# Graph network kernel: zeros of two one-hot tiles by VectorE at the program's start, one input load moved into the preparation, the last count stores on two queues

## The chip, the cores and the metric

The kernel runs on one core of a Trainium2 chip. The metric is the device time of one execution in microseconds, lower being better. Before the change it is 4598.26 us, the median of three runs (4597.88 to 4599.86). A shorter wall time on this one core is all that counts.

The core has five engines that run side by side and wait for each other by semaphores: TensorE (PE, matrix multiplication), VectorE (DVE), ScalarE (ACT), GpSimd (POOL) and SyncE (SP). SP, ACT and POOL also issue DMAs. An engine works through its own instructions in order, so an instruction that waits holds up everything behind it on that engine.

## The reference, cut to what matters

There are 6250 nodes with 128 features (x) and 206250 directed edges (src, dst), sorted by dst. Two layers follow each other, each with a residual and a layer norm:

```
deg  = segment_sum(1, col);  dinv = rsqrt(deg);  w = dinv[row] * dinv[col]
x_out = 0.1 * x;  h = x
for 5 times:  h = segment_sum(h[col] * w, row);  x_out += 0.18 * h
x = layernorm(x + x_out @ weight.T + bias)          # layer 0: propagation
x = layernorm(x + edge_attention(x, edge attributes))  # layer 1: 8 heads, softmax per dst node
```

The change touches only what comes before and at the start of layer 0's five rounds.

## The kernel before, in words

Nodes are held in 49 tiles of 128. Edges are padded to 206336 and laid out so that 1612 of them lie on each of the 128 partitions. The work has four stages, in this order.

**Preparation** (in `gnn_kernel`, lines 1168 to 1243). x goes to the tile `hs` (line 1170), the edges' ends and attributes to SBUF and to DRAM scratch (`srct`, `dstt`, `eat`). DVE makes bf16 one-hot tiles of the destinations (`one_hot`, line 153) and PE multiplies them into the number of edges of each node (line 1206). From this come `cnt`, `first` (the first edge of a node) and `dinv`. Here the framework's scheduler sets the order on each engine.

**Counting** (`count_rows`, lines 158 to 269). It makes a dense matrix of uint8 counts, destination by source, in DRAM (`counts`). POOL gathers the sources of every node's edges by 49 indirect DMAs (line 178), one a node tile. Then POOL writes zeros over the off-diagonal halves of two one-hot tiles `oh_los` (lines 185 and 186), two memsets a tile. These stay zero: for each tile t, DVE writes only the two diagonal blocks of `oh_los[t % 2]` and the whole of `oh_hi`. The loop over t runs in an order written out by hand for PE, DVE and ACT, in a software pipeline: `split` (seven tiles at a time, DVE), `turn` (PE transposes, ACT copies them out), `hot` (DVE one-hots), `count` (64 matmuls into PSUM, line 228, that ACT casts into `cT`, line 230), `put` (DVE transposes `cT` into `c_row`, line 236, adds the self loop, line 243, and SP stores it in 16 DMAs, line 249). `cT` and `c_row` have two buffers each. POOL is not in that hand-written order: after the gathers and the memsets it scales `hs` by `dinv` (line 1253, seven instructions, one of which runs ahead of the gathers).

**The sums** (`propagate`, lines 272 to 465). Five rounds; in each, four quarters of the destination nodes; in each, all 49 source tiles. SP loads two tiles' counts at a time into `c8` (line 419, five buffers). DVE (line 427) and ACT (lines 432 to 440) cast them to fp32r, and PE multiplies them by `parts`, the split `hs` (line 444). `parts` is made by ACT (line 415) and DVE (line 416) during the first quarter of each round. Ahead of all this, ACT issues three loads: `xo` (x again, 3.2 MB, line 287), the weight `wT` (line 288) and the bias (line 289), and scales `wT` (line 290). `xo` is first used when a quarter's sums are finished (line 329). A side job, one step per source tile, orders the nodes and lays out the edges for the next stage.

**Attention** (`attend`), which neither the diff nor the prediction's steps touch.

Each DMA issued by SP or ACT signals one of eight completion counters, which the scheduler hands out in turn over both queues; a DMA waits until the last one on its counter has landed.

Of the kernel before, what the change touches and what calls it, by code (L numbers as in the profile page):

```python
# [7 lines left out]
F32 = mybir.dt.float32  # L8
BF = mybir.dt.bfloat16
FR = mybir.dt.float32r  # L10
U8 = mybir.dt.uint8
# [7 lines left out]
P = 128  # L19
N = 6250  # L20
NT = 49
# [12 lines left out]
D = 128  # L34
# [11 lines left out]
Q = 4  # L46
# [3 lines left out]
H4 = 25  # L50
# [104 lines left out]
        table[:, None, :n, :].to_broadcast([p, b, n, Q]), OP.is_equal)  # L155


def count_rows(tc, first, cnt, srct, tab_lo, tab_hi, iota, ident_b, counts):

    nc = tc.nc
    with tc.tile_pool(name="cr1", bufs=1) as one, tc.tile_pool(name="cr2", bufs=2) as two, \
            tc.tile_pool(name="cr_t", bufs=1, space=PSUM) as pt, \
            tc.tile_pool(name="cr_c", bufs=6, space=PSUM) as pc:
        src = one.tile([P, NT, SLOTS], I32, name="src_e")
        low = one.tile([P, 7, SLOTS], I32, name="low_e")  # L170
        high = one.tile([P, 7, SLOTS], I32, name="high_e")
        ok = one.tile([P, 7, SLOTS], F32, name="ok_e")

        lh = one.tile([P, NT, 4, SLOTS], BF, name="lh")
        at = one.tile([P, NT], I32, name="at_e")
        nc.vector.tensor_copy(at, first)
        for t in range(NT):
            nc.gpsimd.indirect_dma_start(
                out=src[:, t, :], out_offset=None, in_=srct[:, :],
                in_offset=bass.IndirectOffsetOnAxis(ap=at[:, t:t + 1], axis=0))  # L180
        oh_los = [one.tile([P, 64 // Q, P, Q], BF, name=f"oh_l{i}") for i in range(2)]
        cTs = [one.tile([P, H4, 64, 4], U8, name=f"cT{i}") for i in range(2)]
        for i in range(2):

            nc.gpsimd.memset(oh_los[i][:64, :, 64:, :], 0.0)
            nc.gpsimd.memset(oh_los[i][64:, :, :64, :], 0.0)
        turned = {}

        def split(c):

            x = slice(c, c + 7)
            nc.vector.tensor_tensor(ok, iota[:, None, :SLOTS].to_broadcast([P, 7, SLOTS]),
                                    cnt[:, x, None].to_broadcast([P, 7, SLOTS]), OP.is_lt)
            nc.vector.tensor_single_scalar(low, src[:, x], 63, OP.bitwise_and)
            nc.vector.tensor_single_scalar(high, src[:, x], 6, OP.logical_shift_right)
            nc.vector.tensor_copy(lh[:, x, 0:2], low[:, :, None, :].to_broadcast([P, 7, 2, SLOTS]))

            for i in (2, 3):
                nc.vector.scalar_tensor_tensor(lh[:, x, i], ok, -float(P), high, op0=OP.mult, op1=OP.add)

        def turn(t):

            p_t = pt.tile([P, 2, P], BF, name="p_lh")
            for i in range(2):
                nc.tensor.transpose(p_t[:, i, :], lh[:, t, 2 * i:2 * i + 2].rearrange("p a j -> p (a j)"),
                                    ident_b)
            turned[t] = two.tile([P, 2, 64], BF, name="lhT")
            for a in range(2):
                y = slice(64 * a, 64 * a + 64)
                nc.scalar.copy(turned[t][y], p_t[y, :, y])  # L210

        def hot(t):

            v = turned.pop(t)
            for a in range(2):
                y = slice(64 * a, 64 * a + 64)
                one_hot(nc, oh_los[t % 2][y, :, y, :], v[y, 0, :], tab_lo[y], 64)
            oh_hi = two.tile([P, 64 // Q, 4 * H4, Q], BF, name="oh_h")
            one_hot(nc, oh_hi, v[:, 1, :], tab_hi, 4 * H4)
            return oh_hi  # L220

        def count(t, oh_hi):
            cT = cTs[t % 2]
            for q0 in range(0, 64, 5):
                n = min(5, 64 - q0)
                p_c = pc.tile([P, 5, 4 * H4], F32, name="p_c")
                for q in range(q0, q0 + n):
                    nc.tensor.matmul(p_c[:, q - q0], oh_los[t % 2][:, q // Q, :, q % Q],  # L228
                                     oh_hi[:, q // Q, :, q % Q], start=True, stop=True)
                nc.scalar.copy(cT[:, :, q0:q0 + n, :].rearrange("p h q m -> p q h m"),  # L230
                               p_c[:, :n].rearrange("p q (h m) -> p q h m", m=4))

        def put(t):

            c = two.tile([P, 2, H4, 32, 4], U8, name="c_row")
            nc.vector.transpose(  # L236
                c.rearrange("p n h l m -> p (n h l m)").bitcast(F32).rearrange(
                    "p (n h l) -> p n h l", n=2, h=H4),
                cTs[t % 2].rearrange("p h q m -> p (h q m)").bitcast(F32).rearrange(
                    "p (h n i) -> p n h i", n=2, h=H4))  # L240
            m = 2 * ((t + 1) % 2)
            own = c[:, :, (t + 1) // 2, :, m:m + 2]
            nc.vector.tensor_tensor(own, own, ident_b.rearrange("p (m n l) -> p n l m", m=2, n=2), OP.add)
            for a in range(2):
                for b in range(2):
                    y = slice(64 * a + 32 * b, 64 * a + 32 * b + 32)
                    for q, (h0, h1) in enumerate(H4S):
                        w = (h1 - h0) * P
                        nc.sync.dma_start(
                            bass.AP(tensor=counts.tensor,  # L250
                                    offset=counts.offset + (t * P + 64 * a) * HR + 2 * h0 * P + b * w,
                                    ap=[[HR, 32], [32 * HR, 2], [1, w]]),
                            c[y, :, h0:h1].rearrange("p n h l m -> p n (h l m)"))

        with tc.manual_schedule(engines=MANUAL):
            hots = {}
            for t in range(-2, NT + 1):
                if 0 <= t + 2 < NT:
                    if t == -2:
                        split(0)  # L260
                    if (t + 2) % 7 == 3 and t + 6 < NT:
                        split(t + 6)
                    turn(t + 2)
                if 0 <= t + 1 < NT:
                    hots[t + 1] = hot(t + 1)
                if 0 <= t < NT:
                    count(t, hots.pop(t))
                if 0 <= t - 1 < NT:
                    put(t - 1)


def propagate(tc, x, hs, wT0, b0, counts, ident, dinv, x1_d, x1_r, rank_i, side):

    nc = tc.nc
    tiled = "(t p) d -> p t d"
    with tc.tile_pool(name="pr1", bufs=1) as one, tc.tile_pool(name="pr2", bufs=2) as two, \
            tc.tile_pool(name="pr3", bufs=3) as three, tc.tile_pool(name="pr4", bufs=4) as four, \
            tc.tile_pool(name="pr_t", bufs=1, space=PSUM) as pt, \  # L280
            tc.tile_pool(name="pr_a", bufs=7, space=PSUM) as pa:
        xo = one.tile([P, NT, D], F32, name="xo")
        parts = one.tile([P, NT, 2, D], FR, name="parts")
        wT = one.tile([P, D], F32, name="wT")
        bias = one.tile([P, D], F32, name="bias")

        nc.scalar.dma_start(xo, x.rearrange(tiled, p=P))
        nc.scalar.dma_start(wT, wT0)
        nc.scalar.dma_start(bias, rows_of(b0, 0, D))
        nc.scalar.mul(wT, wT, ALPHA)  # L290
# [5 lines left out]
        side = side(spare)  # L296
# [106 lines left out]
        with tc.manual_schedule(engines=MANUAL):  # L403
            for k in range(K):
                for q, (t0, t1) in enumerate(QUARTERS):
# [6 lines left out]
                    for j0 in range(0, NT, 2):  # L412
# [9 lines left out]
                        for j in range(j0, j0 + m):  # L422
                            c = four.tile([P, WQ], FR, name="c")
# [703 lines left out]
def gnn_kernel(ctx, tc, x, srcf, dstx, srcp, dstp, easT, eas, wT0, b0, wq, wdot, w1, b1,  # L1127
               wang, w2, wlin, wout, c_ident, c_iota, c_count, c_dump, c_upto, c_before,
               c_heads, c_sum, out):
    nc = tc.nc  # L1130
# [4 lines left out]
    counts = dram.tile([NT, P, HR], U8, name="counts")  # L1135

    srct = dram.tile([EP, 1], I32, name="srct")
# [5 lines left out]
    x1_d = dram.tile([NP, D], F32, name="x1_d")  # L1143
    x1_r = dram.tile([NP, D], F32, name="x1_r")
# [4 lines left out]
    ident = glob.tile([P, P], F32, name="ident")  # L1149
    nc.sync.dma_start(ident, c_ident)  # L1150
    dinv = glob.tile([P, NT], F32, name="dinv")
    has = glob.tile([P, NT], F32, name="has")
    last = glob.tile([P, NT], I32, name="last")
    cnt = glob.tile([P, NT], F32, name="cnt")
# [12 lines left out]
    with ExitStack() as s:  # L1167

        hs = s.enter_context(tc.tile_pool(name="hs1", bufs=1)).tile([P, NT, D], F32, name="hs")
        nc.scalar.dma_start(hs, x.rearrange("(t p) d -> p t d", p=P))  # L1170
        prep_s = s.enter_context(ExitStack())
        prep = prep_s.enter_context(tc.tile_pool(name="prep", bufs=1))
        work_s = prep_s.enter_context(ExitStack())
        work = work_s.enter_context(tc.tile_pool(name="prep_w", bufs=1))

        dst_i = prep.tile([P, NC], I32, name="dst_i")
        nc.sync.dma_start(dst_i, dstp)
# [4 lines left out]
        nc.sync.dma_start(srct, srcf)  # L1182
        nc.sync.dma_start(dstt, dstx)
        nc.scalar.dma_start(eat, eas)


        tab_lo = prep.tile([P, P, Q], BF, name="tab_lo")
# [60 lines left out]
                                  skip_runtime_bounds_check_because="a count of partitions")  # L1248
        with tc.If(unsorted > 0):
            sort_edges(tc, dram, srcf, dstx, eas, dst_i, first, iota, ident, c_before, srct, dstt, eat)  # L1250
        count_rows(tc, first, cnt, srct, tab_lo, tab_hi, iota, ident_b, counts)
        for c in range(0, NT, 7):
            nc.gpsimd.tensor_tensor(hs[:, c:c + 7], hs[:, c:c + 7],
                                    dinv[:, c:c + 7, None].to_broadcast([P, 7, D]), OP.mult)
# [8 lines left out]
                                   rank_i, flag2)  # L1263
            yield from lay_edges(tc, one, two, rows, srct, eat, src_all, eas_o)

        propagate(tc, x, hs, wT0, b0, counts, ident, dinv, x1_d, x1_r, rank_i, side)
    attend(tc, w1, b1, wang, w2, wlin, wqd, wout, ident, rows, c_iota, src_all, eas_o, x1_d, x1_r, out)
    more = nc.values_load(flag2[0:1, 0:1], min_val=0, max_val=P,
                          skip_runtime_bounds_check_because="a count of partitions")
# [79 lines left out]
```

## Time and profile before

| what | value |
|---|---|
| median of three runs | 4598.26 us |
| the profiled execution, its own time | 4606.73 us |
| its span, first to last instruction | 4604.9 us |
| PE busy | 3785.5 us, 82% of the span |
| DVE busy | 3751.0 us, 81% |
| ACT busy | 2051.8 us, 45% |
| POOL busy | 2353.1 us, 51% |
| granted TensorE clock, mean | 0.931 |

The table of windows has one row for a stretch of the span: busy microseconds of PE, of the weight loads (PEld), of DVE, ACT and POOL, each with its number of instructions, then the granted clock, the DMA engines' busy share and GB/s. By stage it reads, in busy time of the three engines named:

| stretch, us | stage | PE | DVE | POOL | granted clock |
|---|---|---|---|---|---|
| 0 to 206 | preparation, first one-hots | 87.21 | 175.26 | 19.85 | 1.00 |
| 206 to 263 | counting, its start | 0.18 | 11.29 | 46.22 | 1.00 |
| 365 to 465 | counting, in its steady course | 59.67 | 99.10 | 0.00 | 0.66 |
| 785 to 850 | from counting to the sums | 40.91 | 38.58 | 1.58 | 0.79 |
| 850 to 930 | the sums | 80.00 | 73.11 | 0.00 | 1.00 |

A line of the timeline gives the start, the duration, the engine (a "q" behind it is the engine's queue, issuing a DMA or waiting), the line of the kernel, the operation, output<-input with shapes, and how many such instructions were merged; in brackets stands the idle time before it and what ended that.

### The profile page before, as it was taken

To read this page: it belongs to the slowest core of one execution; us is meant where nothing else is said; L and a number is where in the kernel's file an instruction comes from. 1 tells how busy PE (TensorE), PEld (TensorE's weight loads), DVE (VectorE), ACT (ScalarE), POOL (GpSimd) and SP (SyncE) were. 2 spreads that over 40 slices of the span, in tenths; PEclk is the share of its full clock that TensorE was granted. 3 is DMA by queue.
4 is the path that set the end of the run, shared out by engine and by line. 5 is a ranking of instruction groups with operands and counts; after the bars stand their busy time and mean duration, and the time that the engine had idled before them with its cause. 6 is when DMAs were issued, how large, how long until landed. Compare 5 with 4: busy or idle time off the path is not lost.

```text
span 4604.9 us, 73118 instructions
## 1 busy us (share of the span) xinstructions
PE 3785.5 (82%) x24823; PEld 3371.9 (73%) x24823; DVE 3751.0 (81%) x5996; ACT 2051.8 (45%) x4137; POOL 2353.1 (51%) x2343
## 2 busy tenths in 40 slices
PE   4345554997999999999868898987888878888886
PEld 4345554886888888787667788887888868787785
DVE  8769996865787787766649898987988988899887
ACT  0046664644656566464334343443443433444333
POOL 0340000056333344303277777777777777777774
PEclk9986766998999999999989999999999999999898
DMA  8023334555877788765365455554555555555442
GB/s 296 9 50 78 80 78 115 150 155 164 238 229 229 222 233 247 230 174 155 111 125 101 98 102 101 103 99 97 102 100 100 106 97 105 102 103 102 90 100 48
DMA packets 389736, 601.64 MB, mean 131 GB/s; under 512 B 120093, under 2 KB 325205, under 8 KB 378554
## 3 DMA queue, kind: packets, MB, share of 16 engines
q1 hardware_dynamic: 256570, 356.98, 32.0%
q0 software_dynamic: 127056, 204.67, 19.4%
q10 hardware_dynamic: 5728, 35.22, 2.3%
q8 instruction: 201, 3.29, 0.3%
q14 instruction: 181, 1.48, 0.1%
HBM read 491.89 MB, written 132.25 MB: 136 GB/s over the span
## 4 chain that ended last, share of the span: by engine, by line
PE 23%; DVE 11%; DMA 8%; POOL 7%; issue 5%; ACT 1%; SPq 0%; DVEq 0%; POOLq 0%; ACTq 0%
DMA xs<-x_d,src_all 7%; PE p_r L850 6%; POOL xs L788 6%; PE p_k L866 5%; PE p_k L864 3%; DVE mkv L839 3%; DVE kv L871 3%; PE acc L444 3%; PE p_g L831 2%; PE p_x L817 1%; DVE kv L902 1%; DVE kv L909 1%; DVE kv L873 1%; PE p_h L831 1%; POOL x_r L368 1%
## 5 line engine op out<-in xcount | busy, mean ns | idle before, releaser
L788 POOL DMA_INDIRECT xs<-x_d,src_all x1658 | 1676.7, 1011 | 505.5 <-issue 423.1
L444 PE MATMUL acc<-c,parts 128*128 128x512 f32 (+1 forms) x6370 | 1411.1, 382 | 78.9 <-DVE c L427 42.8
L444 PEld LDWEIGHTS acc<-c,parts 128*128 128x128 f32 x6370 | 1154.3, 189 | 305.8 <-DVE c L427 48.9
L427 DVE CAST c<-c 128x1024 fp32r<-128x1024 uint8 x980 | 683.8, 716 | 240.1 <-PE acc L444 196.2
L866 PE MATMUL p_k<-wlin_s,mkv 128*128 128x128 f32 x3316 | 755.4, 310 | 0.0
L440 ACT CAST c<-c 128x512 fp32r<-128x512 uint8 x735 | 456.2, 623 | 561.5 <-PE acc L444 441.9
L864 PE MATMUL p_k<-wlin_s,mkv 128*128 128x64 f32 x3316 | 581.1, 258 | 65.7 <-DVE kv L871 64.8
L850 PE MATMUL p_r<-w_s,r 128*128 128x192 f32 x3316 | 619.9, 330 | 0.0
L850 PEld LDWEIGHTS p_r<-w_s,r 128*128 128x128 f32 x3316 | 571.2, 194 | 34.4 <-issue 0.2
L864 PEld LDWEIGHTS p_k<-wlin_s,mkv 128*128 128x128 f32 x3316 | 523.1, 199 | 95.0 <-DVE kv L871 94.1
L871 DVE TENSOR_TENSOR kv<-rr,p_k 128x768 f32<-128x768 f32 (+2 forms) x443 | 397.1, 898 | 205.6 <-PE p_k L866 189.0
L854 ACT COPY rr<-p_r 128x768 f32<-128x768 f32 (+2 forms) x443 | 335.3, 759 | 476.8 <-PE p_r L850 462.2
L839 DVE TENSOR_TENSOR mkv<-p_g,xT 128x512 f32<-128x512 f32 (+3 forms) x866 | 534.2, 659 | 7.0 <-PE p_g L831 6.9
L866 PEld LDWEIGHTS p_k<-wlin_s,mkv 128*128 128x128 f32 x3316 | 523.5, 199 | 0.0
L228 PE MATMUL p_c<-oh_h,oh_l 128*128 128x100 bf16 x3136 | 301.1, 273 | 263.3 <-DVE oh_h L153 199.5
L833 ACT ACTIVATE r<-p_h,b_s 128x512 f32<-128x512 f32 (+3 forms) x433 | 290.6, 671 | 464.1 <-PE p_h L831 456.4
L228 PEld LDWEIGHTS <-oh_l 128*128 128x128 bf16 x3136 | 289.3, 124 | 272.2 <-DVE oh_h L153 208.0
L668 POOL DMA_DIRECT2D eas_o<-eT_l x252 | 204.9, 816 | 505.2 <-DVE eT_l L662 490.7
L817 PE MATMUL p_x<-ident,xs 128*128 128x128 f32 x1658 | 276.9, 279 | 131.7 <-DMA xs<-x_d,src_all 123.2
L230 ACT CAST cT<-p_c 128x500 uint8<-128x500 f32 (+1 forms) x637 | 306.8, 644 | 118.1 <-DVE c_row L236 61.1
L817 PEld LDWEIGHTS p_x<-ident,xs 128*128 128x128 f32 x1658 | 212.2, 142 | 164.4 <-DMA xs<-x_d,src_all 122.6
L820 ACT COPY xT<-p_x 128x512 f32<-128x512 f32 (+3 forms) x433 | 248.6, 574 | 135.9 <-PE p_x L817 131.9
(195 smaller groups left out, 4524.8 us busy)
## 6 DMA issues: line engine op xcount, KB each, us to landing
c<-counts SPq DMA_DIRECT2D x360, 384.0 KB
ea<-eas_o SPq DMA_DIRECT2D x648, 128.0 KB
c<-counts SPq DMA_DIRECT2D x120, 448.0 KB
eas_o<-eT_l POOLq DMA_DIRECT2D x162, 256.0 KB
counts<-c_row SPq DMA_DIRECT2D x588, 48.0 KB
xs<-x_d,src_all POOLq DMA_INDIRECT x1658
eat<-in_eas ACTq DMA_DIRECT2D x1, 25792.0 KB
counts<-c_row SPq DMA_DIRECT2D x196, 56.0 KB
```

The costliest lines, as they stand in the source:

```text
L228: nc.tensor.matmul(p_c[:, q - q0], oh_los[t % 2][:, q // Q, :, q % Q], oh_hi[:, q // Q, :, q % Q], start=True, stop=True)
L427: nc.vector.tensor_copy(c[:, u:u + 1024].rearrange("p (n b x) -> p n b x", n=2, b=2), r[:, :, v:v + 512].rearrange("p b (n x) -> p n b x", ...
L440: nc.scalar.copy(c[:, 1024:w].rearrange("p (b x) -> p b x", b=2), r[:, :, 512:])
L444: nc.tensor.matmul(a[:, :v - u], parts[:, j, i, :], c[:, u:v], start=(j == 0 and i == 0), stop=(j == NT - 1 and i == 1))
L788: nc.gpsimd.indirect_dma_start(out=xs[g][:, i, :], out_offset=None, in_=x1_d[:, :], in_offset=bass.IndirectOffsetOnAxis(ap=src_all[:, c:c ...
L817: nc.tensor.transpose(p_x[:, i * P:(i + 1) * P], xs[g][:, i, :], ident)
L839: nc.vector.tensor_tensor(mkv[g][:, i, :n].rearrange("p j (b e) -> p b j e", b=4), p_g[:, i, :n * P].rearrange("p (b j e) -> p b j e", b=4 ...
L850: nc.tensor.matmul(p_r[:, i // 2, u:u + DK + D], r[:, i, :], w2_s, start=True, stop=True)
L854: nc.scalar.copy(r2[:, b, :f], p_r[:, b, :f])
L864: nc.tensor.matmul(p_k[:, i // 2, u:u + DK], m[:, 0, i, :], wlin_s[:, :DK], start=True, stop=True)
L866: nc.tensor.matmul(p_k[:, i // 2, u + DK:u + DK + D], m[:, 1, i, :], wlin_s[:, DK:], start=True, stop=True)
L871: nc.vector.tensor_mul(k.rearrange("p (b i) f -> p b (i f)", b=b.stop - b.start), r2[:, b, :f], p_k[:, b, :f])
```

## The change

Three edits are made.

1. The two `oh_los` tiles move out of `count_rows` into the preparation's pool, and their four zero memsets are issued by DVE instead of POOL, in the program's text ahead of all loads of the edges. `count_rows` gets the tiles as an argument.
2. `xo` moves out of `propagate` into a pool of its own beside `hs`. Its load stands in the preparation, on ACT's queue behind the load of `eat`.
3. `c_row` gets three buffers instead of two. Of the last tile's 16 stores (t = 48), the eight of the second half of the partitions (a = 1) are issued by ACT, the others by SP as before.

```
-def count_rows(tc, first, cnt, srct, tab_lo, tab_hi, iota, ident_b, counts):
+def count_rows(tc, first, cnt, srct, oh_los, tab_lo, tab_hi, iota, ident_b, counts):
...
-        oh_los = [one.tile([P, 64 // Q, P, Q], BF, name=f"oh_l{i}") for i in range(2)]
         cTs = [one.tile([P, H4, 64, 4], U8, name=f"cT{i}") for i in range(2)]
-        for i in range(2):
-
-            nc.gpsimd.memset(oh_los[i][:64, :, 64:, :], 0.0)
-            nc.gpsimd.memset(oh_los[i][64:, :, :64, :], 0.0)
...
-            c = two.tile([P, 2, H4, 32, 4], U8, name="c_row")
+            c = two.tile([P, 2, H4, 32, 4], U8, name="c_row", bufs=3)
...
-                        nc.sync.dma_start(
+                        (nc.scalar if a and t == NT - 1 else nc.sync).dma_start(
...
-        xo = one.tile([P, NT, D], F32, name="xo")
-        nc.scalar.dma_start(xo, x.rearrange(tiled, p=P))
...
         nc.scalar.dma_start(hs, x.rearrange("(t p) d -> p t d", p=P))
+        xo = s.enter_context(tc.tile_pool(name="xo1", bufs=1)).tile([P, NT, D], F32, name="xo")
...
+        oh_los = [prep.tile([P, 64 // Q, P, Q], BF, name=f"oh_l{i}") for i in range(2)]
+        for o in oh_los:
+            nc.vector.memset(o[:64, :, 64:, :], 0.0)
+            nc.vector.memset(o[64:, :, :64, :], 0.0)
...
         nc.scalar.dma_start(eat, eas)
+        nc.scalar.dma_start(xo, x.rearrange("(t p) d -> p t d", p=P))
```

In the order of instructions that the scheduler gives the changed kernel, the following differs on the engines. On DVE the four memsets are the first, third, fourth and fifth instruction, and a memset of `ones` and one table operation come a little later. On ACT the load of `xo` stands between those of `eat` and `upto` (a constant that PE needs at the end of the preparation). At the end of counting, ACT's queue has the loads `wq_s`, `wd_s` and `wT`, then the eight stores, then a few small copies, the bias and the scaling of `wT`, and only then the first copy into `parts`. On POOL the memsets are gone, and two loads of x blocks for the last round come ahead of four small set-up operations instead of behind them. Everything else has the same order on all engines.

More of the change, by code (lines that the diff above doesn't have):

```diff
@@ L269, in count_rows, with propagate @@
                     put(t - 1)
-def propagate(tc, x, hs, wT0, b0, counts, ident, dinv, x1_d, x1_r, rank_i, side):
+def propagate(tc, x, hs, xo, wT0, b0, counts, ident, dinv, x1_d, x1_r, rank_i, side):
     nc = tc.nc
@@ L1250, in gnn_kernel @@
             sort_edges(tc, dram, srcf, dstx, eas, dst_i, first, iota, ident, c_before, srct, dstt, eat)
-        count_rows(tc, first, cnt, srct, tab_lo, tab_hi, iota, ident_b, counts)
+        count_rows(tc, first, cnt, srct, oh_los, tab_lo, tab_hi, iota, ident_b, counts)
         for c in range(0, NT, 7):
@@ L1264, in side @@
             yield from lay_edges(tc, one, two, rows, srct, eat, src_all, eas_o)
-        propagate(tc, x, hs, wT0, b0, counts, ident, dinv, x1_d, x1_r, rank_i, side)
+        propagate(tc, x, hs, xo, wT0, b0, counts, ident, dinv, x1_d, x1_r, rank_i, side)
     attend(tc, w1, b1, wang, w2, wlin, wqd, wout, ident, rows, c_iota, src_all, eas_o, x1_d, x1_r, out)
```

## Prediction

> **What bounds the kernel now.** I read the page first (82% PE, 81% DVE: no engine is full, so stages differ), then the table of windows by stage, then the list of waits, longest first in total, then the timeline at the seams between stages. Two seams stand out. The list of waits (engine and line, who ended it, total us, times, longest) has the first:
>
> ```profile
> PE p_c L228 <- POOL oh_l L186: 63.8, 2, 62.9
> DVE oh_l L153 <- PE p_c L228: 51.7, 1, 51.7
> ```
>
> PE once waits 62.9 us for a POOL memset, and DVE once 51.7 us for the matmuls behind it. The timeline shows where:
>
> ```profile
> 198.19 4.61 DVE L153 TENSOR_TENSOR oh_l<-lhT,tab_lo 64x4096 bf16<-64x4096 bf16 x2 [0.68 <-ACT lhT L210]
> 203.92 3.22 POOL L178 DMA_INDIRECT src_e<-srct,at_e  x1 [0.30 <-issue]
> 206.24 4.60 DVE L153 TENSOR_TENSOR oh_l<-lhT,tab_lo 64x4096 bf16<-64x4096 bf16 x2
> 214.27 0.62 DVE L192 TENSOR_TENSOR ok_e<-iota,cnt 128x448 f32<-128x448 f32 x1
> 216.21 1.14 DVE L199 SCALAR_TENSOR_TENSOR lh<-ok_e,high_e 128x448 bf16<-128x448 f32 x2
> ...
> 254.73 0.95 POOL L178 DMA_INDIRECT src_e<-srct,at_e  x1 [0.30 <-issue]
> ...
> 262.82 6.17 PE L228 MATMUL p_c<-oh_h,oh_l 128*128 128x100 bf16 x64 [62.94 <-POOL oh_l L186]
> 269.09 5.99 DVE L153 TENSOR_TENSOR oh_l<-lhT,tab_lo 64x4096 bf16<-64x4096 bf16 x2 [51.74 <-PE p_c L228]
> 269.95 18.60 POOL L1253 TENSOR_TENSOR hs<-hs,dinv 128x896 f32<-128x896 f32 x6
> ...
> 306.34 4.59 DVE L153 TENSOR_TENSOR oh_l<-lhT,tab_lo 64x4096 bf16<-64x4096 bf16 x2
> ```
>
> DVE has the one-hots of tiles 0 and 1 ready at 214.35 and the next split done at 217.35. Then it is idle until 269.09, because PE may not start tile 0's matmuls before POOL's memsets, and POOL reaches those only after 49 gathers. From 304 on DVE is 99% busy at 10.12 us a tile (306.34 to 316.46: 4.6 for oh_l, 3.5 for oh_h, 1.84 transpose, 0.3 add), while PE is busy 60%: counting is bound by DVE, so an earlier start of DVE is an earlier end, one for one. The second seam:
>
> ```profile
> 769.78 18.74 SPq L249 DMA_DIRECT2D counts<-c_row  x40
> ...
> 775.10 1.84 DVE L236 STREAM_TRANSPOSE c_row<-cT 128x1600 f32<-128x1600 f32 x1 [6.74 <-DMA counts<-c_row]
> ...
> 790.08 2.64 SPq L419 DMA_DIRECT2D c<-counts  x5
> ...
> 791.05 16.55 ACTq L288 DMA_DIRECT2D wT<-in_wT  x1
> ...
> 808.13 0.41 ACT L415 CAST parts<-hs 128x256 fp32r<-128x256 f32 x1 [17.96 <-issue]
> ...
> 809.09 3.22 PE L444 MATMUL acc<-c,parts 128*128 128x384 f32 x7 [35.97 <-DVE parts L416]
> ...
> 811.63 0.31 ACT L290 ACTIVATE wT<-wT 128x128 f32<-128x128 f32 x1 [2.08 <-DMA wT<-in_wT]
> ```
>
> SP issues the count stores at 18.74/40 = 0.47 us each; the last starts at 788.1, and the sums' first load goes out at 790.08. ACT issues the load of xo, then needs 16.55 us to issue the small wT behind it, and only then makes the first parts, without which PE cannot start (809.09). It stalls once more at 811.63 for wT itself. After that PE is busy 100% (850 to 930) and nothing in the chain to the end depends on a time before this seam.
>
> **The change part by part.**
>
> *Zeros off POOL.* PE can start tile 0 when oh_h of tile 0 is there (its second DVE operation ends near 206.2), and finishes by 213 (its 64 matmuls take 6.17). DVE's next one-hot then starts at 217.35 instead of 269.09: **51.7 us gained**. The cover that is lost: what POOL did while DVE stood idle now runs beside a full DVE. 32 gathers are left at 215.5. Beside one-hots they took 1.9 to 3.2 us instead of 0.95, seven of them 16.8 us (198.64 to 215.48), 2.4 each with the gaps. So they end near 215.5 + 32 x 2.4 = 292 and not 255. The split that needs gather 20 comes at t = 8, near 217 + 7 x 10.1 = 288; gather 20 is out by 225. Nobody waits. The one-hots were not slowed by the gathers (4.61 and 4.60 at 198 and 206, 4.59 alone at 306). They are slowed by POOL's scaling of hs (5.99 and 7.46 instead of 4.6): from 269.09 the two tiles beside it took 14.15 and 12.98, that is 6.9 us over 2 x 10.12. The same six instructions will meet a full DVE again, later, so the 6.9 us stay in both. Here the Trainium skill speaks against the change: "SBUF — State Buffer", section "The single rule", says VectorE and GpSimd share a port pair by an exclusive lock, a VectorE operation with two SBUF inputs blocking a GpSimd one that reads SBUF for its whole length. By the rule a gather could wait out a whole one-hot (3.5 + 1.25 = 4.7 us), 32 of them until 366; gather 20 would still be out by 235, so the answer is the same. For the six scalings the rule allows 6 x 1.72 = 10.3 us of blocked DVE, against 6.9 in the row. I take the row; bounds: 3.4 lost, 6.9 gained.
>
> *Zeros on DVE.* They cost DVE time at the start of the program, where the timeline has this:
>
> ```profile
> 30.75 1.84 DVE L1238 TENSOR_TENSOR viol<-dflat,dprev 128x1612 f32<-128x1612 int32 x1 [10.61 <-DMA dprev<-in_dstx]
> ```
>
> DVE's chain has 10.6 us to spare there. The built memsets write 2048 four-byte elements each. Nearest row: DVE's memset of 128 in 0.165 us, so at most 4 x 2048 x 1.29 ns = 10.6 us; "VectorE: DVE Perf Modes", section "Zero memsets can be issued as uint32", has one cycle an element, 4 x 2.13 = 8.5 us as an estimate. They start at 0.84; ident_b (0.23) comes among them, tab_lo (0.43) after them, and the first operation on dst_i (6.30 now) starts near 10.2, with tab_hi and ones (0.44) behind it: some 4.4 us late, inside the 10.6. **Nothing** on the path. A gain is excluded, as nothing else starts earlier; were the memsets twice as long (4096 elements), 17 to 21 us would push the chain 2 to 6 us past that wait. Taken 0, bounds 0 and 6 lost.
>
> *xo's load moved.* In the preparation its row-wise descriptors (6272 of 512 B) queue behind eat, whose last packets end at 109.9. At the 325 GB/s of that stretch, 3.2 MB need 10 us more. ACT stands in its issue meanwhile, as it did for 16.47 us behind hs, and upto waits behind it. upto is wanted at 178.7 and ACT's next work at 179.2, so all lands with 50 us to spare; without that cover it would be the 16.5 us. DVE's wait for dprev is not touched: dprev is ahead of eat.
>
> At the seam ACT's path loses 790.15 to 807.6. What is late next is the counts load: the DMA completions in the trace have the first c8 load land at 793.96, 3.88 us after its issue, and xo's packets started only at 794.0, so this is its own time. From ACT's first cast of c8 to PE's first matmul it is 809.09 - 808.44 = 0.65 us. PE starts 4.5 us after that load's issue: 794.6 if stores end as before, **14.5 us gained**. wT, now issued before the last stores, will have landed; the stall at 811.63 delayed the second source tile (PE's first seven matmuls take 3.22 instead of 1.52 for a source tile), so **1.6 us** more. Bounds 12 and 19. POOL's two x loads move ahead of rec_o's set-up; in the built program they wait for no store, so DVE's first use of rec_o is not held up.
>
> *The last stores.* Tile 48's DVE transpose waits 6.74 us for a c_row buffer now; with three it starts at 771.8, when ACT's last cast is done, and ends at 773.9. SP's chain of 0.47 us stores is not shortened by that: it ran without a gap. What shortens it is eight stores less, 8 x 0.47 = 3.8 us. But in the built program SP's seventh store of tile 47 waits on the completion counter of ACT's sixth store. ACT issues wq_s, wd_s, wT from 771.9 and its stores from 774.0; fifth and later wait for the first to land (last store at 788.1, landing seen at 789.8: 1.7 us each), so the sixth lands near 778.1, and SP, due at 776.4, loses 1.7. **2.1 us gained.** The skill's "DMA: Bandwidth & Descriptors", section "Issuing engines are not separate DMA queues", says several issuing engines save only the sequencer's time, usually small beside the DMA. The row says this case is the exception: issue, 0.47 us a store, is what limits. By the rule 0, by the row 2.1; taken 2.1, bounds 0 and 3.8. ACT's stores and copies are over by about 780, before its first parts are needed.
>
> **Sum.** 51.7 + 14.5 + 1.6 + 2.1 = 69.9 us off the profiled execution (span 4604.9, with 1.8 around it 4606.73; that is 0.18% above the median of 4598.26, so the difference carries over): 4598.3 - 69.9 = **4528.4 us**. In the trace of after the first sums' matmul should stand at 809.1 - 69 = 740.
>
> **Rivals.**
> 1. *Contention gives part back.* If each of 32 gathers cost DVE what each scaling did (6.9/6 = 1.15 us), 37 us come back: 4565. Against it: one-hot rows unchanged beside 15 gathers.
> 2. *The sums' start is not freed:* ACT's queue before the first parts grows (three loads, eight stores, bias), or c8 and the counter waits are slower than summed, so that only the first seam counts: 4598.3 - 52 = 4546. For it: parts now stand behind all these. Against: they need some 8 us from 772, and 20 are there.
> 3. *Slower, by the granted TensorE clock.* PE bounds the sums (1411 us in line 444). The clock was granted 1.00 there after two long pauses of PE, but 0.66 in counting and 0.92 to 0.97 in attention. If with the pauses gone the sums ran at the mean of 0.93, they would take 1411 x 0.07/0.93 = 106 us more: 4634. It turns the sign once the clock there falls below 0.953. Against it: the sums run at 1.00 for hundreds of us after the pauses (1200 to 2000).
> 4. *The change doesn't do what it says:* a build that keeps PE waiting for POOL would show 4598 less 18, 4580. Against: the built POOL queue has no memset.
>
> **How the numbers follow.** Likeliest sum 0.76, rival 1 0.06, rival 2 0.10, rival 3 0.03, rival 4 0.01; 0.04 for a gain over 80 us. The range of the likeliest is the bounds of its terms: best 51.7 + 6.9 + 19 + 3.8 = 81, worst 51.7 - 3.4 - 6 + 12 = 54. That gives 4517 to 4544, and taking in rival 2, 4517 to 4547. A measurement tells 0.2% (9 us) from no change. Faster: all but rival 3 and a remainder, 0.95; same 0.02; slower 0.03.
>
> **What would show it.** No wait of PE for POOL in the list; POOL's gathers ending near 290, beside one-hots of 4.6 us; viol still released by dprev near 30.7; PE's first sum 4.5 us after the first c8 issue; SP's queue with one gap of about 1.7 us in tile 47's stores; the granted clock still 1.00 in the sums. I am wrong if one-hots beside the gathers take over 4.7 us for longer than the scalings explain, or if upto lands after 178.

## The result, and the profile after

The changed kernel takes 4538.76 us (median of 4 runs, 4530.61 to 4540.00) against 4598.07 for the kernel before, run beside it (4 runs, 4597.83 to 4599.86): a ratio of 0.9861, 95% interval 0.9848 to 0.9874, or 59.3 us less. The profiled execution took 4539.91 us (span 4538.1), 66.8 less than the profiled one of before. In the changed kernel the lines of counting have numbers 4 or 5 lower than before, and those of the sums 6 lower: the one-hots' matmul is L223, the transpose into `c_row` L231, the stores L245, the load of counts L413, the sums' matmul L438; the scaling of hs is L1254.

The list of waits no longer has POOL in counting. PE now waits for DVE's one-hots, many times and briefly, as it must where DVE is the bound (engine and line, who ended it, total us, times, longest):

```profile
PEld L223 <- DVE oh_h L153: 216.9, 48, 17.0
PE p_c L223 <- DVE oh_h L153: 214.8, 49, 16.8
```

The timeline at the first seam:

```profile
205.88 6.16 PE L223 MATMUL p_c<-oh_h,oh_l 128*128 128x100 bf16 x64 [6.50 <-DVE oh_h L153]
...
215.72 1.14 DVE L194 SCALAR_TENSOR_TENSOR lh<-ok_e,high_e 128x448 bf16<-128x448 f32 x2
...
216.78 4.60 DVE L153 TENSOR_TENSOR oh_l<-lhT,tab_lo 64x4096 bf16<-64x4096 bf16 x2
...
222.50 3.21 POOL L178 DMA_INDIRECT src_e<-srct,at_e  x1 [0.30 <-issue]
...
289.36 0.94 POOL L178 DMA_INDIRECT src_e<-srct,at_e  x1 [0.30 <-issue]
289.49 11.21 DVE L194 SCALAR_TENSOR_TENSOR lh<-ok_e,high_e 128x448 bf16<-128x448 f32 x2
290.33 9.88 POOL L1254 TENSOR_TENSOR hs<-hs,dinv 128x896 f32<-128x896 f32 x6
300.63 4.59 DVE L153 TENSOR_TENSOR oh_l<-lhT,tab_lo 64x4096 bf16<-64x4096 bf16 x2
```

PE starts at 205.88, and DVE's third pair of one-hots at 216.78 instead of 269.09. The gathers run beside one-hots that keep their 4.60 us and end at 290.3. Then comes something that was not in the trace of before: the same two DVE operations that took 1.14 us at 215.72 take 11.21 at 289.49, while POOL runs its six scalings of hs at 9.88/6 = 1.65 us each. Before, the six took 18.60 us, beside one-hots.

At the program's start, DVE alone:

```profile
1.23 1.76 DVE L1173 MEMSET oh_l<- 64x2048 uint32 x1 [1.23 <-PEq L1341]
...
8.03 1.76 DVE L1174 MEMSET oh_l<- 64x2048 uint32 x1 [0.47 <-issue]
...
30.89 1.84 DVE L1239 TENSOR_TENSOR viol<-dflat,dprev 128x1612 f32<-128x1612 int32 x1 [6.85 <-DMA dprev<-in_dstx]
```

The memsets' work fits into the wait for dprev, which is 6.85 us long instead of 10.61 and ends at the same time (30.89 against 30.75). On ACT's queue the issue of `upto` stands behind the loads of `eat` and `xo` until 116.4, and PE first reads `upto` at 178.8:

```profile
24.28 92.14 ACTq L1212 DMA_DIRECT2D upto<-in_c_upto  x1
```

The second seam, on all engines:

```profile
724.65 0.33 ACTq L282 DMA_DIRECT2D wT<-in_wT  x1
...
725.08 6.05 ACTq L245 DMA_DIRECT2D counts<-c_row  x8
...
732.32 0.41 ACT L409 CAST parts<-hs 128x256 fp32r<-128x256 f32 x1
...
741.33 8.54 SPq L413 DMA_DIRECT2D c<-counts  x7
...
745.84 4.46 PE L438 MATMUL acc<-c,parts 128*128 128x384 f32 x14 [13.67 <-DMA c<-counts]
```

ACT's 16.55 us of issue and DVE's wait for parts are gone; PE waits only for the first load of counts and starts 4.51 us after its issue. But ACT needs 6.05 us for eight stores that 3.8 would do, and SP's queue, between 715 and 742 us, has this among its waits:

```profile
SPq L245 <- DMA counts<-c_row: 4.2, 2, 3.2
SPq L245 <- DVE c_row L238: 2.7, 2, 2.5
```

SP's last stores stood 4.2 us for earlier stores to land, 3.2 of it for one of ACT's. Before, the last 40 stores had no gap.

In the sums, 746 to 930 us, the table of windows (busy us of PE, PEld, DVE, ACT and POOL with their instructions, granted clock, DMA share, GB/s) still has a full PE, and a clock of 0.99 on average:

```profile
746.00:930.00 184.00, 184.00 (x882) 155.69 (x883) 151.29 (x435) 103.94 (x262) 45.32 (x42) 0.99 0.54 150
```

The first microseconds of the sums are not at full clock in either kernel (first row before, second row after):

```profile
809.00:820.00 11.00, 10.91 (x47) 9.19 (x48) 8.96 (x31) 8.50 (x31) 0.00 (x0) 0.82 0.59 157
746.00:757.00 11.00, 11.00 (x51) 9.69 (x52) 10.68 (x38) 8.49 (x31) 0.00 (x0) 0.85 0.80 252
```

### The profile page after: what moved, and what is told of

Read it like the earlier page. It is cut to its first block, busy times and chain, and to the rows that moved or that the text cites. A ratio compares the mean times of both kernels' runs of the same rounds, so it can differ in the third digit from the quotient of the medians.

```text
span 4538.1 us, 73113 instructions
## 1 busy us (share of the span) xinstructions
PE 3783.3 (83%) x24823; PEld 3370.0 (74%) x24823; DVE 3762.0 (83%) x6000; ACT 2045.8 (45%) x4137; POOL 2361.9 (52%) x2339
## 3 DMA queue, kind: packets, MB, share of 16 engines
q0 software_dynamic: 127056, 204.67, 19.8%
## 4 chain that ended last, share of the span: by engine, by line
PE 22%; DVE 10%; DMA 8%; POOL 8%; issue 6%; ACT 1%; SPq 0%; POOLq 0%; DVEq 0%; ACTq 0%
DMA xs<-x_d,src_all 8%; POOL xs L782 7%; PE p_r L844 6%; PE p_k L860 5%; PE p_k L858 3%; PE acc L438 3%; DVE mkv L833 3%; DVE kv L865 3%; PE p_g L825 2%; PE p_x L811 1%; DVE kv L896 1%; PE p_h L825 1%; DVE kv L903 1%; DVE kv L867 1%; POOL x_r L362 1%
## 5 line engine op out<-in xcount | busy, mean ns | idle before, releaser
L438 PE MATMUL acc<-c,parts 128*128 128x512 f32 (+1 forms) x6370 | 1410.0, 382 | 53.9 <-DVE c L421 40.0
L438 PEld LDWEIGHTS acc<-c,parts 128*128 128x128 f32 x6370 | 1154.1, 189 | 280.0 <-DVE c L421 44.9
L827 ACT ACTIVATE r<-p_h,b_s 128x512 f32<-128x512 f32 (+3 forms) x433 | 289.9, 670 | 461.4 <-PE p_h L825 454.7
L223 PE MATMUL p_c<-oh_h,oh_l 128*128 128x100 bf16 x3136 | 301.2, 273 | 214.8 <-DVE oh_h L153 214.8
L223 PEld LDWEIGHTS <-oh_l 128*128 128x128 bf16 x3136 | 289.5, 124 | 223.5 <-DVE oh_h L153 216.9
```

The lines of the kernel that those rows point to most:

```text
L438: nc.tensor.matmul(a[:, :v - u], parts[:, j, i, :], c[:, u:v], start=(j == 0 and i == 0), stop=(j == NT - 1 and i == 1))
```

## The experiments

Three places of the trace measure them better than a total does, since a profiled execution moves by ten us in the later stages for no reason that the edits give (the one with edit 2 alone stands 14.5 us early at the seam and 29.0 at its end, while its median is 12.3 lower): tile 8's transpose into `c_row`, the first load of counts, the first matmul of the sums. In the kernel before they are at 367.77, 790.08 and 809.09 us. The table has their shift in us.

| kernel | median us | ratio to before, 95% | tile 8 | first load | first sum |
|---|---|---|---|---|---|
| the change | 4538.76 | 0.9848 to 0.9874 | -49.0 | -48.8 | -63.3 |
| e1_zeros_only | 4548.07 | 0.9873 to 0.9906 | -47.3 | -47.6 | -47.8 |
| e2_x_only | 4585.37 | 0.9957 to 0.9984 | -1.0 | +0.2 | -14.5 |
| e3_stores_only | 4593.79 | 0.9982 to 1.0000 | +0.1 | -1.4 | -1.4 |
| e4_no_stores | 4537.34 | 0.9850 to 0.9883 | -49.1 | -48.5 | -63.1 |
| e5_scale_on_act | 5012.03 | 0.9805 to 0.9882 | -59.5 | -59.2 | -73.7 |
| e6_scale_later | 5033.45 | 0.9846 to 0.9914 | -59.3 | -50.9 | -65.6 |
| e7_stores_pool | 5029.01 | 0.9836 to 0.9907 | -49.5 | -58.4 | -72.6 |
| e8_act_pool | 5015.25 | 0.9800 to 0.9873 | -59.3 | -68.3 | -81.7 |
| r1_after | 4533.77 | 0.9840 to 0.9871 | -48.9 | -48.8 | -63.4 |
| r2_scale_on_act | 4522.06 | 0.9813 to 0.9840 | -59.3 | -58.8 | -73.3 |
| r3_act_pool | 4511.28 | 0.9793 to 0.9820 | -59.3 | -68.7 | -83.2 |
| e9_pool_eight | 4535.85 | 0.9848 to 0.9878 | -49.4 | -50.7 | -65.3 |

e5 to e8 ran on another chip, where the kernel before took 5089.73 us (7 runs); their totals are compared with that only. Beside e1 to e4 it took 4597.71 (17 runs), beside r1 to r3 and e9 4598.47 (9 runs).

### Each edit alone

e1_zeros_only is the changed kernel with edits 2 and 3 undone.

```
-            c = two.tile([P, 2, H4, 32, 4], U8, name="c_row", bufs=3)
+            c = two.tile([P, 2, H4, 32, 4], U8, name="c_row")
-                        (nc.scalar if a and t == NT - 1 else nc.sync).dma_start(
+                        nc.sync.dma_start(
...
-        nc.scalar.dma_start(xo, x.rearrange("(t p) d -> p t d", p=P))
```

(and xo's tile and load as in the kernel before). e2_x_only has edit 2 alone, e3_stores_only edit 3 alone, e4_no_stores is the change without edit 3.

> Only the zeros are moved to VectorE; the x load stays in the sums, the stores and buffers are as before. Theory (terms read from the two traces): this edit alone brings 49 us, 59.2 from the lost wait less 10.2 that VectorE later stands behind GpSimd's six scalings of hs. First sums' matmul near 760 (809.1 before), median near 4549. Rival (the prediction's terms): 51.7 us, first sums' matmul near 757.4, median near 4546.

> Only the load of x for the sums is moved into the preparation. Theory: ScalarE's 17 us of issuing at the sums' start go, the first counts load (3.9 us) and the 0.65 us from cast to matmul take their place: first sums' matmul at 794.6 (14.5 earlier), 15 us in all, median near 4583. Rival: the load slows the preparation (upto lands late, gathers later) and gives part back: counting starts later than 198.2.

> Only the third count-row buffer and the last tile's stores on two queues. Theory: nothing to gain, since SyncE waits for ScalarE's stores through the shared completion counters (a gap of 4.5 us in the trace of after) and that eats what eight fewer stores save: first counts load within 0.7 us of 790.1, median within 1 us of before. Rival (the prediction): 2.1 us earlier, 788.0.

> The changed kernel with two count-row buffers and all stores on SyncE again. Theory: same as the changed kernel; first counts load within 0.7 us of 741.3 and first sums' matmul within 0.7 of 745.8. Rival (the prediction): both 2.1 us later, 743.4 and 747.9.

*Edit 1* brings 49.6 us in the median and 47.8 at the seam (in its profiled execution the preparation ended 1.7 us later than in the change's). Its tile 1 stands 57.5 us early (59.2 in the change), its tile 8 only 47.3: ten are lost between, with edits 2 and 3 absent. The line of the loss is there as in the change:

```profile
291.19 11.21 DVE L194 SCALAR_TENSOR_TENSOR lh<-ok_e,high_e 128x448 bf16<-128x448 f32 x2
```

*Edit 2* brings 14.5 us at the seam, at the step where it was expected. PE then starts 4.3 us after the first load's issue (790.26) and not 19.0:

```profile
794.59 17.65 PE L443 MATMUL acc<-c,parts 128*128 128x384 f32 x82 [22.51 <-DMA c<-counts]
```

It also has a cost that the prediction's sum does not have: its counting stands 1.0 us early at tile 8, its first load 0.2 late. With xo's load gone, ACT issues the load of the bias among the last stores (776.37; before, 807.64), and SP stands 1.5 us for it.

*Edit 3* alone brings 1.4 us at the seam (in the median 3.9, with an interval that reaches 1.0000): neither theory's number. Beside the other two it brings 0.3 us at the first load: e4, without it, has its first load at 741.62 and its first sum at 745.99, the change at 741.33 and 745.84. The waits of SP's queue at the end of counting, in e3 (715 to 790 us):

```profile
SPq L250 <- DVE c_row L243: 15.8, 6, 2.7
SPq L250 <- DMA counts<-c_row: 2.6, 1, 2.6
...
SPq L250 <- DMA wq_s<-in_wq: 0.4, 1, 0.4
```

SP saves 8 x 0.47 = 3.8 us of issue and waits 2.6 + 0.4 = 3.0 for other transfers' counters, where the kernel before waited 0.3. The same waits in e4 (715 to 742 us):

```profile
SPq L245 <- DVE c_row L238: 2.2, 1, 2.2
SPq L245 <- DMA bias<-in_b: 1.2, 1, 1.2
SPq L413 <- DMA counts<-c_row: 0.8, 2, 0.4
```

They come to 4.2 us; in the change it is 4.2 and 2.7, shown above, and the same 0.8 behind them, 7.7 in all. So the edit saves 3.8 us of issue and adds 3.5 of waits, which leaves the 0.3.

### Where ten microseconds of counting went

Theory: POOL's scaling of hs holds DVE, and what that costs depends on the operation it meets. e5_scale_on_act takes the scaling from POOL; e6_scale_later moves it to where DVE makes one-hots, by making it wait for a copy of `dinv` that DVE makes ahead of tile 12's one-hots (all seven, as none can run ahead of the gathers then).

```
-        for c in range(0, NT, 7):
-            nc.gpsimd.tensor_tensor(hs[:, c:c + 7], hs[:, c:c + 7],
-                                    dinv[:, c:c + 7, None].to_broadcast([P, 7, D]), OP.mult)
+        for t in range(NT):                        # e5, ahead of count_rows
+            nc.scalar.mul(hs[:, t], hs[:, t], dinv[:, t:t + 1])
```
```
+                if t + 1 == 12:                    # e6, in count_rows
+                    nc.vector.tensor_copy(late, dinv)
...
-                                    dinv[:, c:c + 7, None].to_broadcast([P, 7, D]), OP.mult)
+                                    late[:, c:c + 7, None].to_broadcast([P, 7, D]), OP.mult)
```

> The changed kernel with the scaling of hs by dinv done by ScalarE, 49 small operations ahead of counting, where ScalarE is idle for some 17 us. Theory (GpSimd's scalings hold VectorE up for 10.1 us): VectorE's two operations on lh near 289 take 1.1 us instead of 11.2, the transposes from tile 8 on stand 59 us ahead of before instead of 49, first sums' matmul near 735.7 (745.8 in the changed kernel), median 10 us lower. Rival (the loss is from something else that ends near 300, such as the last gathers): the 11.2 us stay.

> The changed kernel with all seven scalings of hs made to wait, by a small copy of dinv on VectorE, until the one-hots of tile 12 begin, so that they meet one-hots and not the operations on lh. Theory A (the price depends on what they meet: 1.15 us each beside one-hots, as in the kernel before): 7 x 1.15 = 8 us lost, GpSimd's seven take near 21 us. Theory B (an exclusive lock: each scaling holds VectorE for its whole 1.65 us): 7 x 1.65 = 11.6 us lost, GpSimd's seven take near 11.6 us.

In e5 DVE has its 1.14 us back, and 10.5 us at the seam, though the gathers end at 289.9, as late as in the change (290.3):

```profile
289.09 1.14 DVE L194 SCALAR_TENSOR_TENSOR lh<-ok_e,high_e 128x448 bf16<-128x448 f32 x2
290.15 4.59 DVE L153 TENSOR_TENSOR oh_l<-lhT,tab_lo 64x4096 bf16<-64x4096 bf16 x2
```

ScalarE's 49 scalings take 14.5 us, between 182 and 197, where it stood idle. In e6 the loss moves with the scalings, to tiles 9 to 11, and is smaller: tile 8 is 59.32 us early and tile 12 50.97, 8.35 lost for seven. On POOL and DVE, from two answers of its timeline:

```profile
320.93 22.97 POOL L1257 TENSOR_TENSOR hs<-hs,late 128x896 f32<-128x896 f32 x7 [30.86 <-DVE late L261]
```
```profile
333.41 1.56 DVE L238 TENSOR_TENSOR c_row<-c_row,ident_b 128x128 uint8<-128x128 uint8 x1
334.88 7.46 DVE L153 TENSOR_TENSOR oh_l<-lhT,tab_lo 64x4096 bf16<-64x4096 bf16 x2
342.38 4.86 DVE L153 TENSOR_TENSOR oh_h<-lhT,tab_hi 128x6400 bf16<-128x6400 bf16 x1
```

Here POOL is held up (3.28 us each) and DVE pays some 1.2 us for each (0.30 became 1.56, 3.49 became 4.86). Beside the SCALAR_TENSOR_TENSOR of the split it is DVE that stands, 10.07 us, and POOL that runs at 1.65. What a scaling costs DVE depends on what DVE is doing when it comes: 1.2 us, or all of its own length. The number of e6's theory A, 8, came out; its theory B's 11.6 did not.

### What ate the last stores

Theory: SP and ACT share eight completion counters; GpSimd's DMAs don't wait on these. e7_stores_pool gives GpSimd half of the stores of the last three tiles, e9_pool_eight the eight that ACT has in the change, e8_act_pool is e7 with e5.

```
-                        (nc.scalar if a and t == NT - 1 else nc.sync).dma_start(
+                        (nc.gpsimd if a and t >= NT - 3 else nc.sync).dma_start(     # e7
+                        (nc.gpsimd if a and t == NT - 1 else nc.sync).dma_start(     # e9
```

> The changed kernel with half of the stores of the last three tiles on GpSimd's queue (which has counters of its own) instead of eight on ScalarE's. Theory (SyncE's issue at 0.47 us a store and the shared counters set the end of counting): SyncE has 24 stores left after tile 46 instead of 40, its last goes out near 729 and GpSimd's last near 735; the first counts load near 736 instead of 741.3, first sums' matmul near 740.5. Rival: GpSimd needs 1 us a store and lands them later, first counts load not before 741.

> Both: hs scaled by ScalarE, and half of the last three tiles' stores on GpSimd's queue. Theory: the two gains add, 10 and 5 us: first sums' matmul near 730.5, median 15 us below the changed kernel. Rival: one of the two is hidden behind the other or behind a new wait; the sum is below 10.

> The changed kernel with the eight stores of tile 48 on GpSimd's queue where it has ScalarE's. Theory A (what ate edit 3 is the completion counters that SyncE's and ScalarE's stores share: SyncE's seventh store of tile 47 waits for ScalarE's sixth store): GpSimd's stores are not on those counters, SyncE's chain runs without a gap and has eight stores less, 8 x 0.47 = 3.8 us, so the first count load is issued near 737.8 instead of 741.33. Theory B (any second queue slows the landings from 1.7 to 2.9 us, and that is what ate it): still near 741.3. Total 3.5 below the changed kernel under A, the same under B.

e9 gains 1.5 us at the first load over the change (2.0 less the 0.5 that its whole counting is early), not theory A's 3.5 and not theory B's nothing. The waits of SP's queue say why (715 to 740 us):

```profile
SPq L245 <- DVE c_row L238: 2.5, 1, 2.5
SPq L245 <- DMA bias<-in_b: 1.7, 1, 1.7
...
SPq L245 <- DMA wT<-in_wT: 0.8, 1, 0.8
```

With no store on ACT, SP's stores wait for ACT's loads of wT and the bias, which hold counters of the same eight: 2.5 us of the 3.8. So SP does wait by the counters, but the theory counted only the stores on them. The total did not resolve it (4535.85 against r1's 4533.77, with overlapping ranges).

How long such a wait is depends on when a transfer lands, and theory B's second queue is not what makes stores land late. By the completion times in the traces, the last 40 stores before landed 1.6 to 1.9 us after their issue. In e3, with two queues, none of the last stores took over 2.5. In e2 and e4, with one queue, five stores in a row took 3.6 to 4.5 us: they were issued among POOL's two loads of x and ACT's load of the bias, which in these two runs go out ahead of the last stores, in the kernel before, e1 and e3 behind them. In the change the loads of x go out at 724.92 and 725.74, and the stores issued from 725.08 to 729.22 took 2.6 to 4.4. No run takes these loads away, so how they delay the stores is not shown.

e7 gained 9.7 us at the first load (9.2 without the 0.5 that its counting is early), more than expected:

```profile
716.29 13.70 SPq L245 DMA_DIRECT2D counts<-c_row  x24
731.64 2.68 SPq L413 DMA_DIRECT2D c<-counts  x5
```

SP issues 16 stores fewer than in the change, 7.5 us, and waits 5.7 us instead of 7.7 until the first load, 2.4 of it for DVE's last rows and 2.2 still for the loads of wT and the bias. e8 has both gains, 19.6 us earlier at the first load and 18.5 at the first sum.

### The version that beats both

> The changed kernel once more, so that the three others of this set stand beside it on one chip. Its first count load should be issued near 741.3 us and the first matmul of the sums start near 745.8, as in its first profile. If the ratio to the kernel before leaves the interval 0.985 to 0.987 of its first runs, those runs said less than their interval does.

> The changed kernel with the scaling of hs on ScalarE, ahead of counting, once more. Theory (GpSimd's scalings hold VectorE for 10.1 us): 10 us below the changed kernel of this set, the first matmul of the sums at 735.4. Rival (the time is given back later in the sums, where TensorE's clock sets the pace): the seam is earlier but the total is the same within 4 us.

> Both together, the scaling on ScalarE and half of the last three tiles' stores on GpSimd's queue, once more. Theory (both seams lie on the path and their gains add): 18.5 us below the changed kernel of this set, the first matmul of the sums at 727.3. Rival (the total keeps less than the seam shows): between 5 and 14 us below.

On one chip: the change 4533.77, with the scaling on ScalarE 4522.06 (11.7 less, 9.9 at the seam), with half of the last stores on GpSimd as well 4511.28 (22.5 less, 19.8 at the seam), 0.9806 of the kernel before (0.9793 to 0.9820). The seam of r3:

```profile
706.40 13.41 SPq L245 DMA_DIRECT2D counts<-c_row  x24
706.67 12.85 POOL L245 DMA_DIRECT2D counts<-c_row  x24 [416.61 <-DVE c_row L238]
...
721.38 8.60 SPq L413 DMA_DIRECT2D c<-counts  x7
...
725.94 4.28 PE L438 MATMUL acc<-c,parts 128*128 128x384 f32 x14 [9.80 <-ACT c L429]
```

Neither rival held: what is gained at the seam stays gained to the end.

## Why the prediction was right

The time, 4538.76, lies in the range; the forecast of 4528.4 was 10 us too low. Term by term, at the places of the trace:

- **Zeros off POOL, 51.7: measured 49.0.** The third pair of one-hots came 52.3 us earlier (269.09 - 216.78). The gathers ran beside one-hots of 4.60, and nobody waited for them. That they ended at 290.3, with 292 worked out, is luck: the rows from 198.64 to 215.48 hold six gathers and not seven, so 2.8 us each and an end near 305; in the change the last 32 took 2.35 each, since beside a transpose they were not slowed (the one at 286.75 took 0.95). The step that failed is "the same six instructions will meet a full DVE again, later, so the 6.9 us stay in both", with "I take the row". They met another DVE operation and cost 10.1: 52.3 + 6.9 - 10.1 = 49.1. The rule of the Trainium skill ("SBUF — State Buffer", "Who interferes with whom", the single rule) gave 10.3 for the six (6 x 1.72), and the trace agrees here in size; beside one-hots it does not (e6: 1.2 us a scaling, not all of its length). VectorE stood through all six scalings, though its operation began at 290.02, ahead of the first of them (290.34). So the row taken was right for scalings beside one-hots, but they no longer fell there. By r2, with no scaling on POOL, 59.3 are there.
- **Zeros on DVE, 0: right,** by its cover. All four took 8.56 us from the first start to the last end, which is near the estimate by the skill's page (8.5) only because of the gaps: a memset took 1.76 us, not the 2.13 of the page's cycle an element, and 0.47 of gap followed.
- **xo's load moved, 14.5: measured 14.5** (-63.3 against -48.8 in the change; in e2 14.7 from the first load to the first sum). Its shadow is as wide as argued: ACT's queue stood until 116 and PE wanted upto at 178.8.
- **wT's stall, 1.6: 0.4.** The size was misread from PE's first seven matmuls (3.22 us instead of 1.52). Most of that is the clock: 0.50 was granted from 809 to 811 us before and from 745.84 to 748 after, and a matmul with 512 columns took 628 ns then, 392 to 397 once the clock was 1.00. In the changed kernel, with no wait for wT, the first source tile still took 2.94 us, against 3.24 before. The first pair of source tiles took 4.65 us instead of 5.08, and from the second pair on PE takes 3.01 us a pair in both kernels.
- **The last stores, 2.1: measured 0.3** (e4). The mechanism, a shared counter, was named with 1.7 us; it cost 4.2 (4.3 in r1). ACT's second store, issued at 725.53, was seen landed at 728.78; only then could its sixth go, on the same counter; that was seen landed at 731.64, and SP's store on that counter went at 731.66. The sum had 1.7 us for each of these landings, the trace 3.25 and 2.84: the prediction had seen that POOL's loads of x move ahead, and had no term for their company. The skill's "usually small" ("DMA: Bandwidth & Descriptors", "Issuing engines are not separate DMA queues") had 0 for this term, and 0.3 came, but for another reason: 3.8 us of issue were saved and waits took 3.5 back. On GpSimd's queue, e7 gained 9.2.

Sum: 49.0 + 14.5 + 0.4 - 0.2 = 63.7 against 69.9, where 0.2 is what the shift loses from tile 8 to the first load (49.0 to 48.8). PE stands 63.7 us early at the second pair of source tiles and at the end of the first quarter; the medians say 59.3 and, in r1, 64.7. Where the 4 us between the first median and the seam lie is open; they are within the spread of the changed kernel's runs.

Of the rivals, 1 is refuted for the gathers (no one-hot beside them was longer), yet a smaller contention, by the scalings, was real. 2 is refuted by the first sum. 3 is refuted by the clock of 0.99 in 746 to 930 us and by PE's 1410.0 us in L438, against 1411.1 before. 4 is refuted by the list of waits.

## What to carry to other kernels

When a stall is removed, the work that used to fill it moves beside other work, and its price has to be taken for the neighbour that it will have, not from the row of the neighbour that it had. Before a second queue is given stores, look at what else stands on that queue, which completion counters it shares, and which loads will run beside the stores: ACT's queue gave 0.3 us for eight stores, GpSimd's 1.5 more for the same eight and 9.2 more for 24. Before a slow first stretch is counted as a stall, look at the clock that was granted in it. Large loads that nobody waits for soon belong where their engine's issue can stand still unseen.

## What had not been expected of the hardware

- Six f32 tensor_tensor of GpSimd (128x896) stopped VectorE's f32 scalar_tensor_tensor for 10.07 us while they ran at 1.65 us each; beside bf16 one-hots they took 3.1 to 3.3 us and cost VectorE 1.2 each.
- A small load issued behind two large row-wise ones held ScalarE's queue for 92.14 us, as one behind 3.2 MB alone had done for 16.55.
- The sums' first matmuls ran at a granted clock of 0.50 in six traces (before, the change, e1, e2, e3, r3), for 2.9 to 4.5 us after the first of them began.
- Stores of counts that landed in 1.6 to 1.9 us took up to 4.5 us when they were issued among the loads of x and of the bias (e2, e4), from one queue as from two.
